# Layer 1's attention output product: seven fp32 quarter products become three fp32r products of split operands

## The chip, the cores and the metric

The kernel runs on one core of one Trainium2 chip. The metric is the device time of one execution in microseconds (us); the time before is the median of three runs. Five engines take their instructions in order, each from a queue of its own: TensorE (PE in the profile; PEld is its weight load), VectorE (DVE), ScalarE (ACT), GpSimd (POOL) and SyncE (SP), which here only issues DMAs. They wait for each other by semaphores. The order of the instructions on each engine is that in which the program issues them (`tc.manual_schedule()`).

## What is computed

Two transformer layers with AdaLN over `x` of shape 4 x 512 x 512 in fp32. Layer 0 has a small attention and a masked linear layer. Layer 1 has a causal attention with 32 query heads in 8 groups, each group with one key and value head of 128 columns, and an FFN with integer weights. The change touches layer 1's attention:

```python
q = (hidden_states @ w_q).reshape(B, S, Hkv, g, D)
k = (hidden_states @ w_k).reshape(B, S, Hkv, D)
v = (hidden_states @ w_v).reshape(B, S, Hkv, D)
scores = jnp.einsum('bqhgd,bkhd->bhgqk', q, k) * scale
probs = jax.nn.softmax(jnp.where(causal, scores, -jnp.inf), axis=-1)
attn = jnp.einsum('bhgqk,bkhd->bqhgd', probs, v).reshape(B, S, Hq * D)
return attn @ w_o
```

with B = 4, S = 512, Hkv = 8, g = 4, D = 128; `w_o` is 4096 x 512. The last line is the output product.

## The kernel before

**Blocks, pairs and windows.** Layer 1's attention runs in 32 blocks `n` (L1411): batch `n // 8`, group `n % 8`, four query heads. Two heads make a pair, and one window (L1299) handles a pair: window `2n` is a block's first half, `2n + 1` its second. Window `w` computes the scores of pair `w + 1` and the values of pair `w`, and it fills TensorE with pieces of other products from a list, `fill`, spread over slots 0 to 8 by their costs (`LONG` 1.87, `SHORT` 0.94, `SEVENTH` 1.73): a piece comes in the first slot by whose end its middle is reached.

In slot `i` a window issues, in this order: the transposition of tile `i - 2` on VectorE (`flip`); the division of tile `i - 1` (`divide`: reciprocal on VectorE, multiplication on ScalarE); the score of tile `i` (`score`: product on TensorE, mask and row maximum on VectorE, exponent on ScalarE); in slot 0 `scale_last`; in slots 8 and 9 the values of the pair's two heads (`value`: product on TensorE, eviction on ScalarE); the pieces of `fill`; what `at_slot` names; and the weight steps of `steps`. The eight tiles of a pair have 512, 384, 256, 128 columns, twice. After slot 9, `carry` (L1066) issues 16 DMAs on SyncE that move the pair's probabilities into the layout of the next window's values.

**Split operands.** q, k and v are computed as three fp32r products. A weight w becomes hi, w times a factor a little under one and rounded to fp32r, and lo = w - hi, times 4096. The activation is split in the same way into H, L and a difference D. Piece x (L921, L970) sums hi H + lo L and is evicted by ScalarE; then GpSimd subtracts lo from hi (`less`, L325), and piece p (L936, L983) multiplies what is left with D; VectorE adds it. For q and k, a piece belongs to one head or key and reads 128 columns of hi and lo; each `less` covers one head. For v, x and p belong to two tiles of rows each; both `less` come after the second x, and each covers half the weights' rows.

**Weight steps.** A step (L306) splits one staged tile of 128 x 512 weights: hi on ScalarE, lo on GpSimd, then `scale_last` (the 4096 of the step before, on ScalarE), then the load of a further tile on SyncE into one of four `raw` buffers:

```python
        nc.scalar.mul(hi, w, BELOW)
        nc.gpsimd.tensor_tensor(lo, w, hi.bitcast(F32), SUB)
        scale_last()
        scales.append(((kind, n), lo))
        stage()
```

Three tiles are staged ahead, so a step's load takes the buffer that the step before has just read. Two steps make one operand: `qa` and `qb` (two heads of q each), `k` or `v` (for two blocks). The order is that of `units` (L284): per block k or v, then qa, then qb. In a usual block the steps stand in slots 7 and 8 of the first half (k or v) and in slots 2, 4, 6, 8 of the second.

**The output product.** `o_pieces` (L992) is a 2 x 2 scheme with seven products instead of eight (`seven`, L863): each of the seven pieces multiplies quarters of the block's attention result `oT` and of its 512 rows of `w_o` (`wo`, loaded by one DMA of 1 MB, L232), or sums of quarters, in plain fp32. The sums take four operations on the left (`sums_o`, L882) and four on the right (`sums_wo`, L343), all on GpSimd. A piece is 4 products of 128 x 128 by 128 x 256, shown as 8 instructions. VectorE adds each piece to its own of seven accumulators in `osum` (L880), over the 8 groups of a batch; `leave_attention` (L1123) then combines the seven (7 operations on GpSimd), multiplies by a gate (VectorE) and adds to x (GpSimd).

In a usual block the first half's `fill` holds the four pieces of qa, the four of qb, and the p pieces of k or v begun before; the second half's holds the seven output pieces of block `n - 1` and the x pieces of k or v. After the last block a tail runs its output product, and the FFN follows.

## Time and profile before

| | us |
|---|---|
| three runs | 1956.79, 1956.91, 1956.03; median 1956.79 |
| profiled execution | 1957.64 |
| its span, first to last instruction | 1955.2 |
| windows of layer 1's attention | 168 to about 1620 |
| two windows of block 16 | 910.82 to 932.44, 932.44 to 956.84 |
| layer 0 and setup / FFN | before 168 / from 1641 on |

How to read the profile: a row of a group or of the order of time has the line of the kernel, engine, operation, `out<-in` by the program's names, shapes and a count. In the order of time the first number is the start in us from the span's start, the second the length of the merged row; the bracket at its end is idle time of the engine ahead of it, and who ended it. Product ends are modelled, so rows of TensorE overlap: differences of starts are surer. An fp32 product appears as two instructions, an fp32r one as one (its type is shown as f32 too). SPq rows are DMA issues of SyncE, with the time from issue, or from the start of a wait for its buffer, to the end of the issue. Rows on the tiles `x` and `p` of the names "x<-p" and "x<-x" at L1077 are the moves of `carry`. The table of stages gives, for each stretch, its length, then for PE, PEld, DVE, ACT and POOL the busy time with the number of instructions, the granted clock of TensorE, the DMA share and GB/s.

### The profile page before, as it was taken

To read this page: it belongs to the slowest core of one execution; us is meant where nothing else is said; L and a number is where in the kernel's file an instruction comes from. 1 tells how busy PE (TensorE), PEld (TensorE's weight loads), DVE (VectorE), ACT (ScalarE), POOL (GpSimd) and SP (SyncE) were. 2 spreads that over 40 slices of the span, in tenths; PEclk is the share of its full clock that TensorE was granted. 3 is DMA by queue.
4 is the path that set the end of the run, shared out by engine and by line. 5 is a ranking of instruction groups with operands and counts; after the bars stand their busy time and mean duration, and the time that the engine had idled before them with its cause. 6 is when DMAs were issued, how large, how long until landed. Compare 5 with 4: busy or idle time off the path is not lost.

```text
span 1955.2 us, 27500 instructions
## 1 busy us (share of the span) xinstructions
PE 1926.8 (99%) x8543; PEld 1463.0 (75%) x8543; DVE 1189.5 (61%) x3134; ACT 1101.2 (56%) x2535; POOL 969.9 (50%) x778
## 2 busy tenths in 40 slices
PE   6999999999999999999999999999999999999998
PEld 3446777777777777777777777777777777888887
DVE  7876656656656565565566656656555564755554
ACT  5426766666666666666566666666666562332322
POOL 3335555555558555555675555558555544611010
PEclk9999999999999999999999999999999999999999
DMA  9323555555555556555555555455445456401000
GB/s 326 113 71 120 157 148 165 156 153 146 142 161 162 165 145 161 147 156 151 157 162 169 152 157 136 127 151 160 130 129 156 117 140 230 154 29 36 22 23 23
DMA packets 171932, 269.07 MB, mean 138 GB/s; under 512 B 27266, under 2 KB 95938, under 8 KB 171780
## 3 DMA queue, kind: packets, MB, share of 16 engines
q1 hardware_dynamic: 171252, 266.69, 48.1%
q8 instruction: 71, 1.16, 0.2%
q14 instruction: 81, 0.66, 0.1%
q10 hardware_dynamic: 528, 0.55, 0.1%
HBM read 142.99 MB, written 11.57 MB: 79 GB/s over the span
## 4 chain that ended last, share of the span: by engine, by line
PE 93%; DVE 3%; POOL 1%; SPq 1%; ACT 1%; DMA 1%; issue 1%; POOLq 0%; DVEq 0%
PE quarter L871 20%; PE x L928 15%; PE av L1094 14%; PE sc L1034 14%; PE p L911 9%; PE p_gate L1627 5%; PE p_up L1627 5%; PE acc L1646 4%; PE x L911 3%; PE ffn L761 2%; PE lnT L606 1%; DMA wm<-in_L_wmod_dram 0%; PE narrow L379 0%; PE ffn L765 0%; DVE acc L1131 0%
## 5 line engine op out<-in xcount | busy, mean ns | idle before, releaser
L1037 DVE CUSTOM_DVE_ANT_0 sc<-sc,mask 128x512 f32<-128x512 f32 (+3 forms) x512 | 249.7, 488 | 255.9 <-PE sc L1034 255.9
L1034 PE MATMUL sc<-kT,qT 128*128 128x512 f32 (+3 forms) x1024 | 358.4, 432 | 0.0
L1094 PE MATMUL av<-x,v 128*128 128x512 f32 x1008 | 291.8, 432 | 0.0
L1094 PEld LDWEIGHTS av<-x,v 128*128 128x128 f32 x1008 | 188.3, 189 | 108.4 <-issue 60.8
L1051 ACT ACTIVATE p<-p,sums 128x512 f32<-128x512 f32 (+3 forms) x256 | 143.2, 559 | 128.1 <-DVE sums L1050 127.1
L1034 PEld LDWEIGHTS sc<-kT,qT 128*128 128x128 f32 x1024 | 186.1, 190 | 28.5 <-issue 0.7
L316 POOL TENSOR_TENSOR lo_qa<-raw,hi_qa 128x512 fp32r<-128x512 f32 x64 | 82.6, 1291 | 239.3 <-ACT hi_qa L315 210.4
L997 DVE TENSOR_TENSOR acc<-acc,quarter 128x512 f32<-128x512 f32 x196 | 134.5, 686 | 109.3 <-PE quarter L871 109.1
L1051 ACT ACTIVATE x<-x,sums 128x512 f32<-128x512 f32 (+3 forms) x256 | 142.9, 558 | 81.2 <-DVE sums L1050 81.2
L871 PEld LDWEIGHTS quarter<-wo,oT 128*128 128x128 f32 x720 | 136.5, 190 | 48.5 <-issue 24.4
L871 PE MATMUL quarter<-wo,oT 128*128 128x256 f32 x720 | 170.1, 379 | 0.0
L1054 DVE STREAM_TRANSPOSE p<-p 128x512 f32<-128x512 f32 (+3 forms) x256 | 129.2, 505 | 46.1 <-ACT p L1051 46.0
L1040 ACT ACTIVATE x<-sc,sums 128x512 f32<-128x512 f32 (+3 forms) x256 | 133.4, 521 | 42.2 <-DVE sums L1037 38.7
L1054 DVE STREAM_TRANSPOSE x<-x 128x512 f32<-128x512 f32 x248 | 125.5, 506 | 37.0 <-ACT x L1051 36.4
L1040 ACT ACTIVATE p<-sc,sums 128x512 f32<-128x512 f32 (+3 forms) x256 | 132.0, 516 | 16.2 <-DVE sums L1037 14.5
L316 POOL TENSOR_TENSOR lo_qb<-raw,hi_qb 128x512 fp32r<-128x512 f32 x64 | 82.1, 1284 | 112.3 <-ACT hi_qb L315 108.7
L940 DVE SCALAR_TENSOR_TENSOR qT<-p,qT 128x512 f32<-128x512 f32 x128 | 88.0, 690 | 78.4 <-PE p L911 78.4
L1099 ACT COPY oT<-av 128x512 f32<-128x512 f32 x128 | 74.4, 582 | 85.2 <-PE av L1094 85.2
L326 POOL TENSOR_TENSOR hi_qa<-hi_qa,lo_qa 128x512 fp32r<-128x512 f32 x64 | 82.4, 1288 | 73.0 <-PE x L928 72.7
L326 POOL TENSOR_TENSOR hi_kv<-hi_kv,lo_kv 128x512 fp32r<-128x512 f32 x64 | 81.7, 1290 | 74.2 <-PE x L911 42.6
L326 POOL TENSOR_TENSOR hi_qb<-hi_qb,lo_qb 128x512 fp32r<-128x512 f32 x64 | 82.4, 1287 | 63.2 <-PE x L928 63.2
L871 PE MATMUL quarter<-so,soT 128*128 128x256 f32 x480 | 113.5, 379 | 0.0
(271 smaller groups left out, 4239.3 us busy)
## 6 DMA issues: line engine op xcount, KB each, us to landing
x<-p SPq DMA_DIRECT2D x510, 104.0 KB, 2.2
x<-x SPq DMA_DIRECT2D x493, 104.0 KB, 2.2
raw<-in_L_attn_w_q_dram SPq DMA_DIRECT2D x128, 256.0 KB, 2.9
wo<-in_L_attn_w_o_dram SPq DMA_DIRECT2D x30, 1024.0 KB, 5.7
wm<-in_L_wmod_dram SPq DMA_DIRECT2D x12, 1024.0 KB, 9.9
raw<-in_L_attn_w_k_dram SPq DMA_DIRECT2D x32, 256.0 KB, 3.6
raw<-in_L_attn_w_v_dram SPq DMA_DIRECT2D x32, 256.0 KB, 5.0
xn<-x_d SPq DMA_DIRECT2D x28, 256.0 KB, 4.3
```

Source lines behind the costliest of these rows:

```text
L316: nc.gpsimd.tensor_tensor(lo, w, hi.bitcast(F32), SUB)
L326: nc.gpsimd.tensor_tensor(hi, hi.bitcast(F32), lo.bitcast(F32), SUB)
L871: nc.tensor.matmul(ps[:, m, :], l[:, k, m * P : (m + 1) * P], r[:, k, :], start=(k == 0), stop=(k == 1),)
L911: nc.tensor.matmul(ps[:, m * width : (m + 1) * width], still(l, k, m), moving(r, k), start=(i == 0 and k == 0), stop=(i == len(pairs) - 1 ...
L928: nc.tensor.matmul(banks[j], l[:, k, cols], r[:, k, :], start=(half == k == 0), stop=(half == 1 and k == KC - 1),)
L1034: nc.tensor.matmul(ps[:, :w], q[:, i * P : w], kT[n][:, :w], start=True, stop=True)
L1037: nc.vector.tensor_tensor_reduce(ps[:, :w], ps[:, :w], mask[:, S - w :], -1.0, -NEG, ADD, ALU.min, nmx)
L1040: nc.scalar.activation(blocks(s, i), ps[:, :w].rearrange("p (k j q) -> p k j q", j=NG, q=BK), AF.Exp, bias=nmx, scale=-1.0, accum_out=den,)
L1051: nc.scalar.mul(p, p, rden)
L1054: nc.vector.transpose(blocks(s, i), blocks(s, i))
L1094: nc.tensor.matmul(av.rearrange("p (a i q) -> p a i q", a=NG, q=BK)[:, :, k:], vs[n][:, k, :], moving(k), start=(k == 0), stop=(k == NT - 1),)
L1627: nc.tensor.matmul(ps[kind], w[kind][:, k, c * P : (c + 1) * P], h2[b % 2][i][:, k, :], start=(k == 0 and i == 0), stop=(k == KC - 1 and i ...
```

## The change

The output product takes the form that q, k and v have. The eviction of a value now writes a high part `oH` (ScalarE) and a low part `oL` (VectorE) instead of `oT`; `between_o` makes the difference `oD` on VectorE from the two, head by head, at slot 0 of the two following windows. The rows of `w_o` pass through the weight steps: four more tiles a block, split by ScalarE and GpSimd, and four `less` after the last x piece. `o_pieces` has four x pieces (8 fp32r products of 128 x 128 by 128 x 512) and four p pieces (4 each), one for each tile of 128 rows, all added to one accumulator by VectorE. The sums of quarters, the seven accumulators and their combination go.

The order of the weights becomes k or v, qb of the next block, the output's four, qa of the block after next. A usual block has steps in slots 1, 3, 5, 7, 9, 9 of its first half and 1, 3, 5, 7 of its second. The first half's pieces are qa's and the output's of block `n - 1`; the second half's are qb's and all four of k or v, so their p pieces follow in the same window. In the blocks 6, 14 and 22 the split of the next batch's activations (`swap`) takes a place in the list, and the p pieces of k follow in the next window, at its start. The last block's output product is done in two parts of two heads. One step of layer 0's order (`cs`) is issued earlier.

```diff
@@ -275,6 +240,8 @@
     def unit(kind, n, u):
 
         g = n % HKV
+        if kind == "o":
+            return a["L1_attn_w_o"][g * GW + u * P : g * GW + (u + 1) * P, :]
...
@@ -285,9 +252,16 @@
 
         yield from ((kind, 0, u) for kind in ("k", "qa", "qb", "v") for u in range(2))
         yield from ((kind, 1, u) for kind in ("qa", "qb") for u in range(2))
-        for n in range(NBLK - 2):
-            yield from (("vk"[n % 2 == 0], n // 2 + 1, u) for u in range(2))
-            yield from ((kind, n + 2, u) for kind in ("qa", "qb") for u in range(2))
+        yield from ((kind, n, u) for kind, n in (("k", 1), ("qa", 2)) for u in range(2))
+        yield from (("o", 0, u) for u in range(G))
+        for n in range(1, NBLK):
+            if n + 2 < NBLK:
+                yield from (("vk"[n % 2 == 0], n // 2 + 1, u) for u in range(2))
+            if n + 1 < NBLK:
+                yield from (("qb", n + 1, u) for u in range(2))
+            yield from (("o", n, u) for u in range(G))
+            if n + 2 < NBLK:
+                yield from (("qa", n + 2, u) for u in range(2))
...
+            dst = w if key[0] == "o" else w.rearrange("p (k n) -> p k n", n=W2)
+            nc.sync.dma_start(dst, unit(*key))
...
+        tag = kind if kind[0] in "qo" else "kv"
+        size = KC * W2
+        if kind == "o" and n + 1 == NBLK:
+            tag, n, u = ("qa", "qb")[u // 2], (n, u // 2), u % 2
+        elif kind == "o":
+            size = G * E
         if (kind, n) not in forms:
             forms[kind, n] = tuple(
-                T["wp"].tile([P, KC * W2], F32R, tag=f"{i}{tag}", name=f"{i}_{tag}")
+                T["wp"].tile([P, size], F32R, tag=f"{i}{tag}", name=f"{i}_{tag}")
...
+    def rows_o(n, h):
+
+        u = h
+        if n + 1 == NBLK:
+            n, u = (n, h // 2), h % 2
+        assert all(key != ("o", n) for key, _ in scales), n
+        return [f[:, u * E : (u + 1) * E] for f in forms["o", n]]
...
-    Lt.3 wl lm.3 le.3 F.1.2 ws ld.3 fs.2.0 fa.0.3/d F.2.1/mm hit.3 qs.3 fs.1.2 cs rs ws re fa.2.0/d
+    Lt.3 wl lm.3 le.3 F.1.2 ws ld.3 fs.2.0 fa.0.3/d F.2.1/mm hit.3 cs qs.3 fs.1.2 rs ws re fa.2.0/d
...
-    def seven(still, moving, take, order):
-
-        def piece(i):
-            l, r = still()[i], moving()[i]
-            tiles = l.shape[2] // P
-            ps = bank([P, tiles, r.shape[2]], "quarter")
-            for m in range(tiles):
-                for k in range(2):
-                    nc.tensor.matmul(
-                        ps[:, m, :], l[:, k, m * P : (m + 1) * P], r[:, k, :],
-                        start=(k == 0), stop=(k == 1),
-                    )
-            take(i, ps)
-
-        return [(SEVENTH, lambda i=i: piece(i)) for i in order]
...
+    osum = accp.tile([P, NT + NT // 2, E], F32, tag="acc", name="acc")
+    oH, oL, oD = {}, {}, {}
+
+    def between_o(n, h):
+        if n not in oD:
+            oD[n] = at.tile([P, G, S], F32R, tag="Do", name="o_df", bufs=1)
+        nc.vector.scalar_tensor_tensor(
+            oD[n][:, h], oL[n][:, h].bitcast(F32), -STEP, oH[n][:, h].bitcast(F32), ALU.mult, ADD
...
+    def o_pieces(n, all_heads=tuple(range(G))):
+
+        first_ = n % HKV == 0 and all_heads[0] == 0
+
+        def sums(t, pairs, name):
+            ps, rows_ = bank([P, 512], name), slice(t * P, (t + 1) * P)
+            for i, (l, r) in enumerate(pairs):
+                for h in all_heads:
+                    nc.tensor.matmul(
+                        ps, l[:, h, rows_], rows_o(n, h)[r],
+                        start=(i == 0 and h == all_heads[0]),
+                        stop=(i == len(pairs) - 1 and h == all_heads[-1]),
+                    )
+            return ps
+
+        def x(t):
+            ps = sums(t, ((oH[n], 0), (oL[n], 1)), "x")
+            if first_:
+                nc.scalar.mul(osum[:, t], ps, ONE)
             else:
-                nc.vector.tensor_tensor(osum[:, i - 1], osum[:, i - 1], ps, ADD)
-
-        order = (1, 2, 4, 7, 5, 6, 3) if n + 2 != NBLK else (1, 2, 3, 7, 5, 6, 4)
-        order = (1, 7, 6, 2, 4, 5, 3) if n % HKV == 0 else order
-        return seven(lambda: left["o", n], lambda: right["o", n], take, order)
+                nc.vector.scalar_tensor_tensor(osum[:, t], ps, ONE, osum[:, t], ALU.mult, ADD)
+            if t == NT - 1:
+                for h in all_heads:
+                    less(*rows_o(n, h))
+
+        def p(t):
+            ps = sums(t, ((oD[n], 0),), "p")
+            nc.vector.scalar_tensor_tensor(osum[:, t], ps, -TINY, osum[:, t], ALU.mult, ADD)
+
+        c = len(all_heads) / G
+        return [(c * LONG, lambda t=t: x(t)) for t in range(NT)] + [
+            (c * SHORT, lambda t=t: p(t)) for t in range(NT)
+        ]
...
-            oT[n] = at.tile([P, G, S], F32, tag="oT", name="oT")
+            oH[n] = at.tile([P, G, S], F32R, tag="Ho", name="o_hi", bufs=1)
+            oL[n] = at.tile([P, G, S], F32R, tag="Lo", name="o_lo", bufs=1)
...
-        nc.scalar.copy(
-            oT[n][:, h, :].rearrange("p (i a q) -> p a i q", a=NG, q=BK),
-            av.rearrange("p (a i q) -> p a i q", a=NG, q=BK),
-        )
+        H, L = (t[n][:, h, :].rearrange("p (i a q) -> p a i q", a=NG, q=BK) for t in (oH, oL))
+        av = av.rearrange("p (a i q) -> p a i q", a=NG, q=BK)
+        nc.scalar.mul(H, av, BELOW)
+        nc.vector.tensor_tensor(L, av, H.bitcast(F32), SUB)
...
+        dfs = [[lambda h=h: between_o(n - 1, h) for h in (2, 3)] if behind else []]
+        dfs.append([lambda h=h: between_o(n, h) for h in (0, 1)])
...
-            sums, ends = leave_attention(b - 1, nc.gpsimd, gap, "ga", xb)
-            in_b = {8: sums[:3]}
+            ends = leave_attention(b - 1, nc.gpsimd, gap, "ga", xb)
+            in_b = {0: ends[:1], 2: ends[1:3], 4: ends[3:5], 6: ends[5:7], 7: ends[7:]}
...
-            window(2 * n, o[:2] + t[:2] + [r[0]] + o[2:3] + t[2:3] + [r[1]] + t[3:] + [r[2]] + o[3:4] + [r[3]] + o[4:])
+            fill = o[:2] + t[:1] + o[2:4] + t[1:2] + r[:1] + t[2:3] + r[1:2] + o[4:5] + t[3:] + r[2:3]
+            fill += o[5:6] + r[3:] + o[6:]
+            window(2 * n, fill, (), (1, 3, 5, 7, 8), {0: dfs[0]})
             warm = small.tile([P, 1], F32, tag="warm", name="warm", bufs=1)
             nc.scalar.activation(warm, ones[:, 0:1], AF.Sigmoid)
 
-            last = [f for _, f in o_pieces(n)]
-            s = at.tile([P, 3, 2, HALF], F32, tag="soT", name="soT", bufs=1)
-            A11, A21, A12, A22 = quarters(oT[n])
-            left["o", n] = {1: A11, 2: A12, 3: s[:, 2], 4: A22, 5: A21, 6: s[:, 1], 7: s[:, 0]}
-            nc.vector.tensor_tensor(s[:, 0], A11, A21, SUB)
-            run(last[0], last[3])
+            run(*dfs[1])
+            head, tail = (o_pieces(n, hs) for hs in ((0, 1), (2, 3)))
+            run(*(f for _, f in head[:4]))
             value(NBLK * G - 2)
             value(NBLK * G - 1)
-            nc.vector.tensor_tensor(A21, A21, A22, ADD)
-            nc.vector.tensor_tensor(s[:, 1], A21, A11, SUB)
-            nc.vector.tensor_tensor(s[:, 2], A12, s[:, 1], SUB)
-            run(*last[1:3], *last[4:])
+            run(*(lambda h=h: between_o(n, h) for h in (2, 3)))
+            run(*(f for _, f in head[4:] + tail))
...
-        so = sums_o(n - 1) if n > 0 else 4 * [(0.0, lambda: None)]
-        wo = [(0.0, lambda: sums_wo(n - 1))] if n > 0 else []
         if n == 0:
             window(0, begun[:1] + qa[:1] + begun[1:] + qa[1:] + qb[:1], side[0], (1, 7, 8), {3: [scale_last]}, (9, 9))
         else:
-            fill = begun[:1] + qa[:1] + so[:1] + qa[1:2] + begun[1:] + so[1:2] + qb[:1] + qa[2:3] + so[2:3]
-            fill += qb[1:2] + so[3:] + qa[3:] + wo + qb[2:]
-            window(2 * n, fill, side[0], (7, 8) if more and n % HKV != 1 else (), in_a)
+            fill = begun + qa[:1] + o[:4] + qa[1:3] + o[4:] + qa[3:]
+            early_ = (0, 1, 2, 3, 5, 7) if n == 1 else (1, 3, 5, 7) if more else (1, 3)
+            if n == 1:
+                fill = begun + qa + o
+            in_a.setdefault(0, []).extend(dfs[0])
+            window(2 * n, fill, side[0], early_ + (9, 9), in_a)
...
+        swap = []
         if g == HKV - 2 and after:
             h3[after] = H, L, D
-            for c in range(KC):
-                in_b.setdefault(c, []).append(lambda c=c: (upper(h3[after], spare, c), lower(h3[after], spare, c)))
-                in_b.setdefault(c + 1, []).append(lambda c=c: between(h3[after], c))
+            swap = [(0.0, lambda c=c: (upper(h3[after], spare, c), lower(h3[after], spare, c))) for c in range(KC)]
...
-        fresh = (2, 3, 7, 8) if n == 0 else (0, 1) * (n % HKV == 1) + (2, 4, 6, 8)
-        window(2 * n + 1, (qb[1:] if n == 0 else o) + kv[:2], turns_ + side[1], fresh if more else (), in_b)
-        begun = kv[2:]
+        in_b.setdefault(7 if n == 0 else 0, []).extend(dfs[1])
+        fresh = (2, 3, 6, 7) if n == 0 else (1, 3, 5, 7)
+        late = 2 if n == 0 or swap else len(kv)
+        window(2 * n + 1, (qb[1:] if n == 0 else qb + swap) + kv[:late], turns_ + side[1], fresh, in_b)
+        begun = kv[late:]
...
```

Not shown: the removal of `load`, `quarters`, `left_sums`, `right_sums`, `load_parts`, `rooms`, `sums_wo`, `sums_o`, of the old `o_pieces` and of the seven sums in `leave_attention`; where the last pair's transposed probabilities lie (`straight_of`); names of buffers.

## The prediction, on record before the result was known

> **What bounds the kernel now.** I read the page's top first, then two stages of the attention in the table of stages, then TensorE's order of time, then the queues of ScalarE, GpSimd and SyncE around one border of two windows.
>
> ```profile
> span 1955.2 us, 27500 instructions
> PE 1926.8 (99%) x8543; PEld 1463.0 (75%) x8543; DVE 1189.5 (61%) x3134; ACT 1101.2 (56%) x2535; POOL 969.9 (50%) x778
> PE 93%; DVE 3%; POOL 1%; SPq 1%; ACT 1%; DMA 1%; issue 1%; POOLq 0%; DVEq 0%
> ```
>
> TensorE is the bound. The profiled execution took 1957.64 us: its span and 2.4 us around it; it is 0.85 us over the median of the three timed runs, 1956.79. The table of stages shows windows 32 and 33 (block 16) with no idle TensorE at all (length, then each engine's busy time):
>
> ```profile
> 910.82:932.44 21.62, 21.62 (x99) 16.35 (x97) 12.44 (x38) 13.36 (x33) 16.47 (x14) 1.00 0.59 165
> 932.44:956.84 24.40, 24.40 (x107) 19.09 (x106) 13.55 (x41) 15.38 (x37) 10.23 (x9) 1.00 0.59 167
> ```
>
> The clock is 1.00. A saving on TensorE therefore counts in full, and so does any wait that the change brings it. TensorE's order of time gives the prices; I take them from start to start, since the modelled ends overlap:
>
> ```profile
> 915.12 0.59 PE L1034 MATMUL sc<-kT,qT 128*128 128x256 f32 x2
> 915.37 1.28 PE L928 MATMUL x<-h_hi,hi_qa 128*128 128x512 f32 x4
> 916.48 1.09 PE L928 MATMUL x<-h_lo,lo_qa 128*128 128x512 f32 x4
> 917.41 0.38 PE L1034 MATMUL sc<-kT,qT 128*128 128x128 f32 x2
> ...
> 933.30 1.89 PE L871 MATMUL quarter<-wo,oT 128*128 128x256 f32 x8
> 935.02 0.81 PE L1034 MATMUL sc<-kT,qT 128*128 128x384 f32 x2
> ```
>
> A quarter product is 935.02 - 933.30 = 1.72. Scores take 0.86, 0.65, 0.43 and 0.22 for 512 to 128 columns (932.44 to 933.30 is the first). So an x piece, two of the three products, is 917.41 - 915.12 - 0.43 = 1.86 (others 1.83), and a p piece, the third, 0.94 (925.12 to 926.28 less 0.22).
>
> **The saving.** Per block, 7 quarters at 1.725 = 12.08 go; 4 x at 1.84 and 4 p at 0.935 = 11.1 come. That is 0.98 less, for 31 blocks (the first has no output product behind it; the last one's runs in the tail): **-30 us**. Without new waits a first-half window would be 25.4 us and a second-half one 19.9.
>
> **Work that lies beside TensorE.** GpSimd loses 8 sums per block (soT, oT, so, wo rows) and gains 4 splits and 4 subtractions for the output weights, all at 1.28 to 1.30: 10.3 for 10.3. ScalarE gains 8 passes at 0.62, one every 0.52: 28.7 busy of 46 becomes 33 of 45. VectorE loses 7 sums at 0.69 and gains 4 low parts, 4 differences, 8 accumulations: 26 becomes 32. SyncE issues four loads of 256 KB (0.4 to 0.5 each) where it issued one of 1 MB (0.58). No engine's sum becomes the bound; leave_attention's 7 sums on GpSimd and the cselb move (rsel waits 1.1 us for it now) are worth 1 us at most. What counts is where the new steps stand in the queues.
>
> **The queues as the trace shows them.** ScalarE, GpSimd and SyncE over the border at 932.44, after a window whose last two weight steps stood at its end:
>
> ```profile
> 929.12 0.64 ACT L315 ACTIVATE hi_kv<-raw 128x512 fp32r<-128x512 f32 x1
> 933.58 0.63 ACT L304 ACTIVATE lo_kv<-lo_kv 128x512 fp32r<-128x512 f32 x1 [3.82 <-POOL lo_kv L316]
> 934.11 0.57 ACT L1099 COPY oT<-av 128x512 f32<-128x512 f32 x1
> 934.58 0.69 ACT L1040 ACTIVATE p<-sc,sums 128x512 f32<-128x512 f32 x1
> 935.16 0.20 ACT L1040 ACTIVATION_READ_ACCUMULATOR p<-sc,sums 128x1 f32 x1
> 935.25 0.63 ACT L304 ACTIVATE lo_kv<-lo_kv 128x512 fp32r<-128x512 f32 x1
> ```
> ```profile
> 932.27 2.51 POOL L316 TENSOR_TENSOR lo_kv<-raw,hi_kv 128x512 fp32r<-128x512 f32 x2
> ```
> ```profile
> 922.89 11.05 SPq L298 DMA_DIRECT2D raw<-in_L_attn_w_q_dram  x2
> 934.05 1.15 SPq L1077 DMA_DIRECT2D x<-x  x2
> ```
>
> The second step's scale_last blocks ScalarE until GpSimd's first low part is done (933.54); the exponent of the new window goes ahead of the last scale; the raw load waits 10 us for that same low part, and the 16 moves of the probabilities stand behind it, 1.6 us late. Today it costs nothing: quarters follow. The change moves two steps behind the last value (slot 9, twice) and puts the q, k and v pieces right behind.
>
> **Wait 1, start of the first half, from F.** The block's last step (slot 7 of the window before) splits the second half of the weights of qa, and its scale comes only at the window's start, behind the exponent. qa's first x piece stands in slot 0 and reads that low part with its seventh matmul: F + 0.86 + 6 x 0.23 = 2.25. ScalarE: eviction of the second value from F + 0.20 (911.02 after 910.82), 0.59; VectorE's new low part, 0.61 to the next start; maximum 0.70 + 0.14; exponent 0.68; scale 0.62, ends at F + 3.6. Wait 1.3. Ends: 0.9 (if the maximum could start at 1.06 as at 911.88), 1.5 (a weight load of 0.19 behind it). Blocks 2 to 30 but the 3 after a swap, where k's p pieces lie first: 26 x 1.3 = **+34**.
>
> **Wait 2, second half, from E.** ScalarE: eviction E + 0.2, hi, scale, hi up to 2.24; wait for GpSimd's low part (1.37 to 2.64); scale to 3.2; exponent to 3.88; second scale (low part done 3.91) to 4.5; x eviction, division, exponent to 6.13; hi of slot 1's step to 6.75. GpSimd: that low part to 8.1, and only then the subtraction for qb's second head, to 9.4. Its p piece is due at 0.86 + 1.86 + 0.65 + 0.43 + 1.86 + 0.22 + 0.94 + 0.86 = 7.7. Wait 1.7. Even if GpSimd were in time, the moves would not be: the raw load waits for 2.64, the moves start at 3.2, 16 at 0.635 end at 13.4 and land 2.2 later, 15.6, and the first value is due at 14.6: 1.0. Above, the two new differences of low and high part on VectorE, both read from SBUF, meet GpSimd there. The view of line 1131, the gate, also two such inputs:
>
> ```profile
> L1131 DVE TENSOR_TENSOR acc<-acc,ga x16: 678/1602/1783, 608.6 to 1675.3; 128x512 f32<-128x512 f32 x16
> ```
>
> Alone it takes 0.68, beside GpSimd's work mostly 1.6. Two such collisions delay the low part and then the division by some 0.55: 2.3. I take 2.0; ends 1.0 and 2.5. Windows of blocks 1 to 29: 29 x 2.0 = **+58**.
>
> The Trainium skill, "SBUF — State Buffer", section "Who interferes with whom", says that a VectorE instruction with two SBUF inputs shuts out a GpSimd instruction that reads SBUF, and the reverse, for a whole instruction. The row agrees (0.68 against 1.60); it speaks against this change, whose 128 new differences are all of that kind. With the rule in full wait 2 is 2.3 (29 x 2.3 = 67 us), without it 1.7 (49 us).
>
> **Wait 3, second half, blocks with v (odd).** v's two subtractions follow its second x piece; now they run at 908.25 to 910.75, 4.0 us after that piece began (906.7), and a value of 2.16 and a score of 0.86 cover them. Afterwards only a score of 0.22 lies between. p may start at 2.13, gets its first weights at 2.8 and the rest at 4.05, and ends at 4.77 instead of 3.09: 1.7. If slot 5's low part is ahead on GpSimd, 2.3. I take 1.9: 15 x 1.9 = **+28**.
>
> **Once each.** Window 2 has four steps and qa's products close together, and the output's four subtractions behind one score (+3); in the tail the last p pieces wait for two subtractions of 1.28 (+2): **+5**, ends 0 and 10. In other blocks the four subtractions need 5.0 us from the last x piece's start and 6.4 lie before the last one's use: nothing.
>
> **Sum.** No wait can fall below nothing, since TensorE never stands still now. -30 + 34 + 58 + 28 + 5 = +95 on 1957.6: 2052.6; less 0.85, about **2050 us**. All low ends: -30 + 23 + 29 + 24 + 0 = +46, 2003. All high ends: -30 + 39 + 73 + 35 + 10 = +127, 2084.
>
> **Rivals.**
> A, the other side: the waits are hidden and TensorE's sum decides, -30 + 2: 1929. For it: TensorE stands still nowhere today, and all other engines have 27% or more to spare. Against it: each wait is a chain of measured durations from a window's own border, so spare time elsewhere cannot shorten it. It decides if the three waits together come to less than 0.98 us a block, which is what a block saves.
> B: GpSimd's queue is met in a kinder order, and waits 2 (its part beyond the moves, 29) and 3 (28) go; wait 1 and the moves' 1.0 stay: -30 + 34 + 29 + 5 = +38, 1995. For it: GpSimd is busy only 58% of a block. Against it: the low part of slot 1 is issued ahead of the subtraction.
> C: the time is kept within 0.2% (what a measurement can tell from no change) because only wait 1 comes: -30 + 34, 1960.
>
> **Chances.** Forecast (2003 to 2084) 0.66, B 0.16, C 0.04 (a third of it over 0.2%), A 0.14. Faster 0.14, same 0.03, slower 0.83. With B, the range is 1975 to 2085.
>
> **What would show it.** Right: in the second product's x piece TensorE idles for the scale of lo_qa in each first-half window (about 26.7 us long); in the second half it idles at p for hi_qb and, in odd blocks, hi_kv (windows near 22 and 24 us); moves start 3 us into second halves. Wrong: windows of 25.4 and 19.9 us, TensorE without idle time.

## The result, and the profile after

The changed kernel takes **2199.89 us** (median of 4 runs, 2192.84 to 2200.85), the kernel before 1956.85 in the same comparison (4 runs, 1956.03 to 1957.54): ratio **1.1234**, 95% interval 1.121 to 1.1259. The forecast was 2050, with a range up to 2085. The profiled execution took 2198.98 us, 2.2 more than its span, and 241.3 more than the one of before.

The top of the page, and the first line of the chain that ended last:

```profile
span 2196.8 us, 27560 instructions
PE 1986.6 (90%) x8287; PEld 1436.3 (65%) x8287; DVE 1382.3 (63%) x3411; ACT 1237.7 (56%) x2808; POOL 966.6 (44%) x754
PE 14%; DVE 0%; ACT 0%; issue 0%
```

TensorE was busy for 99% of the span and is now for 90%. It has 256 instructions fewer, and still its busy time is 60 us longer. Matmuls that ran at half clock count double (107 us of the busy time lie in such stretches, 7 before), and the last product ahead of each wait counts with its whole modelled length. The granted clock over the span fell from 0.998 to 0.971.

The table of stages, with the length first, then the busy time of TensorE, its weight loads, VectorE, ScalarE and GpSimd, and the granted clock as the third number from the right. The first two rows are windows 20 and 21 (block 10), the last two windows 47 and 55:

```profile
710.48:737.20 26.72, 25.57 (x106) 18.80 (x105) 16.80 (x46) 15.20 (x36) 12.63 (x10) 1.00 0.50 133
737.20:759.43 22.23, 20.43 (x82) 14.37 (x81) 14.07 (x39) 16.41 (x40) 12.57 (x10) 1.00 0.60 157
1429.85:1454.62 24.77, 20.97 (x106) 15.79 (x105) 14.64 (x40) 17.59 (x42) 13.46 (x10) 1.00 0.47 123
1639.94:1666.36 26.42, 22.61 (x106) 16.71 (x105) 14.63 (x40) 17.59 (x42) 13.47 (x10) 0.94 0.43 115
```

The regular windows are near what the prediction wanted to see (26.7, 22 and 24). Windows 47 and 55 do the same work with the same waits, but 55 takes 1.65 longer: its clock is 0.94.

**Wait 1** in TensorE's and ScalarE's order of time, at the border 710.48. In brackets stands the idle time before an instruction and what ended it:

```profile
712.27 0.62 PE L882 MATMUL x<-h_lo,lo_qa 128*128 128x512 f32 x2
714.04 0.73 PE L882 MATMUL x<-h_lo,lo_qa 128*128 128x512 f32 x2 [1.15 <-ACT lo_qa L279]
```
```profile
712.70 0.69 ACT L1017 ACTIVATE x<-sc,sums 128x512 f32<-128x512 f32 x1 [1.42 <-DVE sums L1014]
713.28 0.19 ACT L1017 ACTIVATION_READ_ACCUMULATOR x<-sc,sums 128x1 f32 x1
713.37 0.62 ACT L279 ACTIVATE lo_qa<-lo_qa 128x512 fp32r<-128x512 f32 x1
```

The third matmul on the low part waits for the scale, which stands behind the exponent.

**Wait 2** in window 21, TensorE, then GpSimd, then VectorE:

```profile
744.43 1.02 PE L1011 MATMUL sc<-kT,qT 128*128 128x512 f32 x2
747.10 1.19 PE L865 MATMUL p<-h_df,hi_qb 128*128 128x512 f32 x4 [1.65 <-POOL hi_qb L306]
```
```profile
738.65 2.98 POOL L296 TENSOR_TENSOR lo_o<-raw,hi_o 128x512 fp32r<-128x512 f32 x2 [5.49 <-issue]
741.59 1.74 POOL L306 TENSOR_TENSOR hi_qb<-hi_qb,lo_qb 128x512 fp32r<-128x512 f32 x1
744.54 1.27 POOL L296 TENSOR_TENSOR lo_o<-raw,hi_o 128x512 fp32r<-128x512 f32 x1 [1.22 <-ACT hi_o L295]
745.77 1.27 POOL L306 TENSOR_TENSOR hi_qb<-hi_qb,lo_qb 128x512 fp32r<-128x512 f32 x1
```
```profile
739.24 2.93 DVE L837 SCALAR_TENSOR_TENSOR o_df<-o_lo,o_hi 128x512 fp32r<-128x512 f32 x2
```

The second subtraction for qb stands behind the low part of slot 1's step (744.54). While VectorE makes its two differences (2.93), the first subtraction takes 1.74; the later one, alone, 1.27.

**Wait 3** in window 55, TensorE, then GpSimd:

```profile
1655.77 0.39 PE L1011 MATMUL sc<-kT,qT 128*128 128x128 f32 x2
1657.40 0.50 PE L865 MATMUL p<-hi_kv,h_df 128*128 128x256 f32 x2 [1.25 <-POOL hi_kv L306]
1658.64 1.47 PE L865 MATMUL p<-hi_kv,h_df 128*128 128x256 f32 x6 [0.74 <-POOL hi_kv L306]
```
```profile
1654.83 1.30 POOL L296 TENSOR_TENSOR lo_qa<-raw,hi_qa 128x512 fp32r<-128x512 f32 x1 [3.56 <-ACT hi_qa L295]
1656.09 2.50 POOL L306 TENSOR_TENSOR hi_kv<-hi_kv,lo_kv 128x512 fp32r<-128x512 f32 x2
```

v's two subtractions stand behind the low part of slot 5's step (1654.83), and v's first p piece waits for each of them in turn.

**Where the time went.** I went through TensorE's order of time from start to start, gave each instruction its usual price, called what is left over a wait for the operand that the view names, and kept the half-clock stretches apart. The prices are medians, so a term is good to 1 or 2 us. Over the spans (+241.6):

| term | predicted | measured |
|---|---|---|
| work saved | -30 | -29 |
| wait 1 | 34 | 39 |
| wait 2 | 58 | 74 |
| wait 3 | 28 | 39 |
| window 2, waits | 3 | 11 |
| window 62 and tail | 2 | 18 |
| other waits | 0 | 50 |
| half clock, up to window 61 | 0 | 44 |
| before window 2, FFN | 0 | -4 |

The other waits have places of their own. At three batch ends (windows 17, 33, 49) VectorE stood 10 us for a load, and TensorE 5.1 to 5.5 of these behind VectorE. TensorE, VectorE and SyncE in window 17:

```profile
647.06 2.07 PE L882 MATMUL x<-h_hi,hi_kv 128*128 128x512 f32 x4 [5.47 <-DVE qT L894]
```
```profile
644.97 0.69 DVE L1114 TENSOR_TENSOR acc<-acc,ga 128x512 f32<-128x512 f32 x1 [10.00 <-DMA ga<-rows]
```
```profile
630.82 10.08 SPq L1057 DMA_DIRECT2D x<-x  x16
640.94 0.59 SPq L154 DMA_DIRECT2D ga<-rows  x1
```

The gate's row is asked for at the second half's start, but SyncE issues the 16 moves first. In window 62 ScalarE stood 10.5 us for a low part that GpSimd could not make, since its casts of the FFN's first weights, ahead in its queue, waited 17.2 for their load:

```profile
1836.34 1.29 POOL L1267 CAST first<-raw 128x512 fp32r<-128x512 int32 x2 [17.20 <-DMA raw<-in_L_ffn_gate_wqT_dram]
1842.18 2.48 POOL L296 TENSOR_TENSOR lo_qb<-raw,hi_qb 128x512 fp32r<-128x512 f32 x2
```

Further: in blocks 3, 11, 19 and 30 o's first p piece waits 3.0 us. A layer norm stands in VectorE's and ScalarE's queues there (L1142, L1154), so ScalarE is late with the hi of slot 3's step; its low part is ahead of o's four subtractions on GpSimd, which begin 16.3 us into window 6 and 13.1 into the regular window 20. Behind the three swaps of the batch the first x piece of k waits 1.5 to 2.4. In window 61 the value product waits 4.9 for the moves.

### The profile page after: what moved, and what is told of

The parts are those of the page before. It is cut to its first block, busy times and chain, and to the rows that moved or that the text cites. A ratio compares the mean times of both kernels' runs of the same rounds, so it can differ in the third digit from the quotient of the medians.

```text
span 2196.8 us, 27560 instructions
## 1 busy us (share of the span) xinstructions
PE 1986.6 (90%) x8287; PEld 1436.3 (65%) x8287; DVE 1382.3 (63%) x3411; ACT 1237.7 (56%) x2808; POOL 966.6 (44%) x754
## 5 line engine op out<-in xcount | busy, mean ns | idle before, releaser
L1075 PE MATMUL av<-x,v 128*128 128x512 f32 x1008 | 312.1, 455 | 4.9 <-DMA x<-x 4.9
L296 POOL TENSOR_TENSOR lo_o<-raw,hi_o 128x512 fp32r<-128x512 f32 x124 | 172.0, 1398 | 238.0 <-issue 144.6
L1083 DVE TENSOR_TENSOR o_lo<-av,o_hi 128x512 fp32r<-128x512 f32 x128 | 88.3, 690 | 226.8 <-ACT o_hi L1082 226.5
L1082 ACT ACTIVATE o_hi<-av 128x512 fp32r<-128x512 f32 x128 | 76.0, 597 | 218.7 <-PE av L1075 218.7
L954 PE MATMUL x<-hi_o,o_hi 128*128 128x512 f32 x496 | 165.1, 455 | 1.2 <-ACT acc L964 1.2
L954 PE MATMUL p<-hi_o,o_df 128*128 128x512 f32 x496 | 145.5, 422 | 14.7 <-POOL hi_o L306 14.0
L296 POOL TENSOR_TENSOR lo_kv<-raw,hi_kv 128x512 fp32r<-128x512 f32 x64 | 83.3, 1302 | 169.4 <-ACT hi_kv L295 161.6
L306 POOL TENSOR_TENSOR hi_o<-hi_o,lo_o 128x512 fp32r<-128x512 f32 x124 | 155.7, 1287 | 3.2 <-PE x L954 3.2
L954 PE MATMUL x<-lo_o,o_lo 128*128 128x512 f32 x496 | 133.7, 391 | 0.0
L865 PE MATMUL p<-h_df,hi_qb 128*128 128x512 f32 x256 | 78.7, 429 | 58.8 <-POOL hi_qb L306 57.7
```

The costliest lines, as they stand in the source:

```text
L306: nc.gpsimd.tensor_tensor(hi, hi.bitcast(F32), lo.bitcast(F32), SUB)
L954: nc.tensor.matmul(ps, l[:, h, rows_], rows_o(n, h)[r], start=(i == 0 and h == all_heads[0]), stop=(i == len(pairs) - 1 and h == all_heads ...
L1075: nc.tensor.matmul(av.rearrange("p (a i q) -> p a i q", a=NG, q=BK)[:, :, k:], vs[n][:, k, :], moving(k), start=(k == 0), stop=(k == NT - 1),)
L1083: nc.vector.tensor_tensor(L, av, H.bitcast(F32), SUB)
```

## The experiments

Two theories stood at first. **A**: each wait is a matter of order, goes when the late work is put earlier or the asking later, and the clock's halves follow from the waits. **B**: the forms can't be made faster by the engines behind TensorE, so a wait taken away comes back at the next place. The expectations use their own letters: the W of e1 and e2 is A; rival A of e1 and E of e5 say that the new products, or their load, lower the clock; C and D belong to e4 and e5 alone.

**e1, wait 1 alone.** The scale of lo_qa at the end of the window before:

```diff
+        if n > 0:
+            in_b.setdefault(9, []).append(scale_last)
```

> Changed kernel, with the scale of the last weight step issued in slot 9 of the second half, ahead of the next window's exponent. Theory W (the loss is waits in the order of the queues): the wait of qa's first x piece, 1.43 us in 27 first halves, goes and nothing takes its place: 39 us less, about 2160; first halves 25.3 instead of 26.7. Rival A (fp32r products of this shape, or the load they put on TensorE, are slow in themselves and lower its clock): no wait moves the time, within 8 us of 2200.

2159.67 us, 40 less, as W said. The same kind of first half, TensorE, without the wait; such a window takes 25.30:

```profile
1582.27 1.49 PE L882 MATMUL x<-h_hi,hi_qa 128*128 128x512 f32 x4
1583.60 1.08 PE L882 MATMUL x<-h_lo,lo_qa 128*128 128x512 f32 x4
```

Wait 1 is order alone: nothing came back.

**e2, wait 2 alone.** The second half's steps one slot later:

```diff
-        fresh = (2, 3, 6, 7) if n == 0 else (1, 3, 5, 7)
+        fresh = (2, 3, 6, 7) if n == 0 else (2, 4, 6, 8)
```

> Changed kernel, with the second half's steps in slots 2, 4, 6, 8 instead of 1, 3, 5, 7, so that the subtraction of qb's second head is ahead of a split on GpSimd. Theory W: wait 2 falls from 2.4 to 1.0 or less (the moves of the probabilities are then what is late), 29 x 1.4 = 40 less; wait 3 falls from 2.5 to 1.7 in 15 windows, 12 less; with the clock's share 10 to 20 more: 2130 to 2150. Rival B (the second half is short of GpSimd's or ScalarE's time as a whole): the wait moves to another piece of the same window, within 10 us of 2200.

2145.91 us, 54 less. The two subtractions now run back to back on GpSimd (1646.60 to 1649.6), and qb's second p piece has no wait in view:

```profile
1646.60 3.01 POOL L306 TENSOR_TENSOR hi_qb<-hi_qb,lo_qb 128x512 fp32r<-128x512 f32 x2
1651.38 1.28 POOL L296 TENSOR_TENSOR lo_o<-raw,hi_o 128x512 fp32r<-128x512 f32 x1 [1.78 <-DMA x<-x]
```

Added up, wait 2 fell from 74 to 12 us and wait 3 from 39 to 31; x pieces of k and v at batch ends and swaps rose by 15, k's p pieces by 7. So the step's low part ahead of the subtraction was the cause; some 30% of the gain came back, as B says.

**e3, the p pieces of k and v a window later.**

```diff
-        late = 2 if n == 0 or swap else len(kv)
+        late = 2
```

> The two p pieces of k or v always stand at the start of the next block's first half, as they already do at n = 0 and at the batch ends. Theory A (wait 1 is there because qa's first x piece opens the first half; wait 3 is there because v's p piece comes right behind its x pieces): both go, 39 + 39 us by the trace of the changed kernel, and the p pieces of k and v at the new place wait some 0.8 us each for hi_kv, 30 places, +24 at most; with less idle time the clock's share of 44 shrinks by some 10. Together about 2199 - 60 = 2140 us, between 2120 and 2160. Rival theory (the work that is late is late wherever it is asked for): 2190 to 2210.

2141.99 us, as A said: waits 1 and 3 both go (78 us), and new ones come: k's p pieces +8, scores at the batch ends 15, and value products that wait for the moves 13, since the second half is now only 21 to 22 us long.

**e4, the collision of VectorE and GpSimd.** The second half's two differences at slot 4:

```diff
-        in_b.setdefault(7 if n == 0 else 0, []).extend(dfs[1])
+        in_b.setdefault(7 if n == 0 else 4, []).extend(dfs[1])
```

> Changed kernel, with the second half's two differences on VectorE in slot 4 instead of slot 0. Theory C (SBUF inputs of VectorE and GpSimd shut each other out at the border): wait 2 falls from 2.4 to about 1.8, 29 x 0.6 = 17 less, 2180. Rival: the chain of ScalarE sets it alone, wait 2 stays 2.4, within 5 us of 2200.

2216.08 us, 16 *more*: both numbers missed. The collision itself did go. GpSimd at the start of one second half, with the first subtraction at 1.31 and not 1.74, and VectorE's two differences in another, 1.28 and not 2.93:

```profile
1710.70 2.52 POOL L296 TENSOR_TENSOR lo_o<-raw,hi_o 128x512 fp32r<-128x512 f32 x2 [5.50 <-issue]
1713.18 1.31 POOL L306 TENSOR_TENSOR hi_qb<-hi_qb,lo_qb 128x512 fp32r<-128x512 f32 x1
```
```profile
1668.75 1.28 DVE L837 SCALAR_TENSOR_TENSOR o_df<-o_lo,o_hi 128x512 fp32r<-128x512 f32 x2
```

Wait 2 fell by some 15 us, 0.5 per window: that is the collision's share of it. (In window 21 ScalarE waits 0.39 for the second low part, which holds up the hi of slot 1's step; here that wait is gone.) But everything behind slot 4 became later: wait 3 rose by 9, the x pieces of k and v at batch ends and swaps by 8, k's p pieces by 8, the half clock by 7. B holds in this run.

**e5, the clock.** Eight products that nobody reads, ahead of qb's second p piece and of v's first one, where TensorE would wait:

```diff
+        def spin(piece):
+            ps, hs = ps_av.tile([P, 512], F32, tag="av", name="spin"), h3[b][0]
+            for k in range(2 * KC):
+                nc.tensor.matmul(ps, hs[:, k % KC, :P], hs[:, k % KC, :], start=True, stop=True)
+            piece()
```

> Changed kernel, with 8 products more (1.87 us of TensorE, into a bank that nobody reads) ahead of qb's last p piece in the second halves, and 8 more ahead of v's first p piece: inside waits 2 and 3 (2.4 and 2.5). The output stays the reference's. Theory D (TensorE's clock is halved for 3.4 or 6.8 us where it stood still too long): the added work costs nothing and keeps the clock at 1: 44 us are lost to the clock now, some 25 to 35 of them after these two waits, so 2165 to 2180. Rival E (the clock falls because of load): the time does not fall, 2200 or more.

2188.57 us: with more work the kernel is 11 us faster, though D's 2165 to 2180 is missed. A regular second half with v, which took 24.8 to 25.0 or 26.4 to 26.7, now takes 24.8 to 25.1; only windows 11, 27 and 43 take longer (27.0, against 29.5 to 29.8):

```profile
1628.54:1653.38 24.84, 24.26 (x122) 18.73 (x121) 14.65 (x40) 17.60 (x42) 13.53 (x10) 1.00 0.46 123
```

The half clock's cost fell from 44 to 22 us; half of that was lost again in places where the eight products are longer than the wait or meet none (window 61 grew from 22.0 to 26.1). Idle TensorE, not the new products, lowers the clock: e11, with all the new products and few waits, has no half-clock stretch at all from window 2 to window 61.

**e6, the two late loads.**

```diff
-            in_b = {0: ends[:1], 2: ends[1:3], 4: ends[3:5], 6: ends[5:7], 7: ends[7:]}
+            in_a.setdefault(4, []).extend(ends[:1])
+            in_b = {2: ends[1:3], 4: ends[3:5], 6: ends[5:7], 7: ends[7:]}
...
-            first_weights()
...
-            window(2 * n, fill, (), (1, 3, 5, 7, 8), {0: dfs[0]})
+            window(2 * n, fill, (), (1, 3, 5, 7, 8), {0: dfs[0], 9: [first_weights]})
```

> Two DMAs asked for earlier or later, nothing else: the gate's row of a finished batch is loaded in the block's first half and not behind the 16 moves of the second half's start, and the first weights of the next stage are loaded and cast at the end of the last window but one. Theory A (at three batch ends VectorE waits 10 us for that row, and TensorE 5.4 of these through k's x piece; and in window 62 TensorE waits 10 us for casts that GpSimd holds back): 3 x 5.4 + 10 and the clock's halves around them, some 8: 2199 - 34 = 2165, between 2155 and 2180. Rival theory (these stalls only show time that another wait would take anyway): within 8 us of 2199.

2166.97 us, 33 less, as theory A said.

**e7, all at once.** e1, e2 and e6, `late = 2`, and these orders of pieces:

```diff
+            fill = qa[:1] + begun + o[:4] + qa[1:2] + o[4:] + qa[2:]
...
+            fill = begun + qa[:2] + o[:4] + qa[2:] + o[4:]
...
+            fill = qb[:2] + kv[:1] + qb[2:] + kv[1:2]
```

> All places at once: the scale of lo_qa at the end of the second half, the second half's steps one slot later, k's first x piece between qb's x and p pieces, the p pieces of k and v in the next first half behind qa's first x piece, the gate's row earlier, the casts later, window 2 with o's x pieces ahead of qa's p pieces. Theory A (the change is worth 30 us of TensorE work and everything else is waits that are a matter of order): the windows without a wait give 1927, and what is left is window 2 (some 8), block 30's moves (5), the swaps (5) and a dozen waits under 0.5 us, with a little clock: 1945 to 1985. Rival theory (the engines behind TensorE, GpSimd with the shared port above all, can't deliver the forms at this pace): over 2040.

2123.74 us: in the rival's range (over 2040) and far from A's 1945 to 1985, but not for the rival's reason. Waits 1, 2 and 3 were gone and GpSimd held up little (18 us, most of it at o's p pieces), but a new one stood in every second half, 106 us in all. TensorE and SyncE of window 21:

```profile
721.04 0.38 PE L1011 MATMUL sc<-kT,qT 128*128 128x128 f32 x2
724.90 2.40 PE L1075 MATMUL av<-x,v 128*128 128x512 f32 x8 [3.48 <-DMA x<-x]
```
```profile
712.31 0.38 SPq L273 DMA_DIRECT2D raw<-in_L_attn_w_q_dram  x1
712.82 10.25 SPq L1057 DMA_DIRECT2D x<-x  x16
```

The half is now 18 us of work, and TensorE reaches the value product 12 us into it. The moves start 3.3 us into it, because a raw load ahead of them waits for GpSimd, and take 10.2.

**e8 and e9, two ways round the moves.** Both put the two value products behind all pieces; e8 issues 4 of the 16 moves on ScalarE's queue, e9 takes the p pieces of k and v back into the second half:

```diff
+        aside = {0: 2, 1: 3, 2: 0, 61: 6}.get(pair, 4 * (pair % 2))
```

> The kernel with all waits out, whose second halves then waited 3.5 us each for the last of the 16 moves of the exponentials (one queue issues them, 0.63 us each). Here ScalarE's queue issues 4 of the 16 in second halves, both value products come behind all of the half's pieces, the steps of the first half stand at slots 1, 2, 5, 7, and the first half behind a swap begins with k's p pieces. Theory A (the moves are the next bound: they can't start before the last value product of the half before has read its tile, and take 10.1 us + 2): 4 moves fewer take 2.5 us off, k's second x piece ahead of the value products another 1.9, so the wait goes: 2124 - 106 and of the clock's 49 most: 1965 to 2010. Rival theory (what ends late is the transfers themselves, not their issue on one queue): the moves still land at the same time and only the 1.9 us of the moved piece are won, 30 x 1.9 + some clock: 2040 to 2070.

> As the run beside it, but the 16 moves stay on one queue, and the p pieces of k and v go back to the second half, behind qb's: work instead of the wait for the moves. Theory A: the second half has 16.3 us of pieces and scores ahead of the value products, 15.3 are needed; what comes back is v's p piece waiting for GpSimd, 1 to 1.7 us in 15 blocks, and k's by some 0.5: 1960 to 2010 with the clock. Rival theory (as beside): the same, since here the transfers' end is hidden by work: it can't tell them apart by itself, only the pair can.

2111.30 and 2045.76 us, both over what was expected, e8 even over its rival's 2040 to 2070. In e8 the wait for the moves went, but issuing is not free on ScalarE: 3.85 us for four, and the first exponent stands behind it:

```profile
712.72 3.85 ACTq L1057 DMA_DIRECT2D x<-x  x4
716.68 0.69 ACT L1017 ACTIVATE p<-sc,sums 128x512 f32<-128x512 f32 x1 [3.39 <-DMA x<-x]
```

In e9 no regular half waits for the moves, and wait 3 is back (2.1 in blocks with v); in those with k the p piece waits 0.8, now for ScalarE's kT.

**e10, the moves first at the border.** e7, with the first half's last two steps at slot 8 in place of 9 and its second one a slot earlier, the value products behind all pieces, and two of o's x pieces first behind a swap:

> The kernel with all waits out, with three changes of order and the moves on one queue again: the first half's last two steps stand at slot 8 and not 9, so that no load of raw weights waits on SyncE's queue ahead of the 16 moves at the border; both value products of second halves come behind all pieces; the first half behind a swap begins with two of o's x pieces. Theory A (the wait for the moves is a matter of 1.3 us by which the load ahead of them is late and of 1.9 us by which k's second x piece stood behind the wait): no wait for the moves is left in the regular blocks; with window 2 (6), the swaps (3 x 3), block 30 (6) and some clock 1950 to 1990. Rival theory (a half of 18 us is too short for the moves' 10.1 us, the flips before them and the landing behind them, whatever the order): 1 to 2 us a block stay, with the clock's halves 2010 to 2060.

2007.37 us. A regular second half has no wait left: SyncE starts the moves 0.2 us into it, and it takes 18 us.

```profile
678.21 10.54 SPq L1057 DMA_DIRECT2D x<-x  x16
```
```profile
1487.15:1505.16 18.01, 18.01 (x90) 13.77 (x89) 12.06 (x37) 14.62 (x37) 8.44 (x7) 1.00 0.61 159
```

The total missed A's range by 17: 24 us for lo_qa's scale were not in the estimate, and the swaps, put at 9, cost 15 at o's x pieces alone. B's "1 to 2 us a block stay" at the moves is wrong.

**e11 to e14, what was left.** e11: the second half's steps at slots 1, 3, 5, 7 again, and a swap's four differences in the next first half. e12: `fill = qa[:1] + begun + o[:4] + qa[1:3] + o[4:] + qa[3:]` and other orders at the swaps, in block 30, in window 2 and in the tail. e13 and e14: window 2 alone, e13 with steps at (0, 0, 1, 2, 5, 7), e14 at (0, 0, 1, 4, 7, 8).

> The kernel with the moves first at the border, with two changes of order: the second half's steps at slots 1, 3, 5, 7 again (so qa's lower form is done a slot sooner), and behind a swap of the batch the four differences of the new x are made in the next first half, where the first p piece asks for them, and not in the second half. Theory A (what was left at 2007 are waits of order: 24 us for lo_qa's scale in first halves, 15 us behind the three swaps, 9 us of clock behind these): 24 and 12 of these go, with the clock some 6: 1960 to 1975; the work alone would give some 1935. Rival theory (the forms can't be made faster: what is won at lo_qa comes back at qb's p pieces as wait 2): 1990 to 2010.

> The kernel with the forms earlier (1968), with what its trace still shows as waits put in another order: qa's first p piece ahead of o's p pieces in first halves (some 25 waits of 0.2 us for GpSimd, 5); in window 2 qa's first x piece first and one step two slots later (6 of waits, some 4 of them); behind a swap one x piece of o between the differences and k's p pieces, and the swap's and block 30's second halves with later steps (1.9 x 3 + 1.5 x 3 + 2); at the very end the second two heads' x pieces between the first two heads' p pieces (2). Theory A (order is all that is left, and the new products' own work is 0.75 us a block shorter than the seven): 1968 - 17 = 1951, between 1946 and 1957, so level with the kernel before or up to 0.5% faster. Rival theory (each of these waits hides another one behind it): 1963 to 1970.

> The kernel ordered all over, with window 2 the other way round again (k's p pieces first, o's x pieces ahead of qa's p pieces) and its first steps earlier (slots 0, 0, 1, 2, 5, 7 and the last scale at slot 3), so that o's lower forms are there when its first x piece is. Theory A (window 2's 39 us, 11.6 more than its work, were the order's fault, 6 of them o's p pieces behind GpSimd's four subtractions; with the regular blocks at 45.1 against 46.1 the whole is level with the kernel before): window 2 falls to 29 to 32, 1965 - 8 = 1957, between 1953 and 1960. Rival theory (window 2 can't be faster, since the weights of o and v come late from memory): window 2 stays above 33, 1960 to 1966.

> As the run before, with the last three single steps of window 2 at slots 4, 7, 8 in place of 2, 5, 7, and the scale before them at slot 2. The trace of the run before shows why window 2 stayed at 35.4: ScalarE stood 6.0 us in its second step on v for a load of raw weights that SyncE issues behind the 16 moves, and o's x pieces stood 4.1 behind ScalarE. Theory A (order again): the 4.4 us for o's x piece go, the clock's 1.4 in that window too, and 1 of the 1.5 for lo_o: 1960 - 6 = 1954, between 1951 and 1957, level with the kernel before or 0.2% faster. Rival theory (the late load only moves the wait to qb's forms in window 3, whose steps now come last): 1957 to 1962.

1968.50, 1965.20, 1959.82 and 1960.91 us, with ratios 1.0061 (1.0047 to 1.0074), 1.0048 (1.0034 to 1.0061), 1.0018 (1.0009 to 1.0027) and 1.0022 (1.0012 to 1.0031). e11 hit. e12 missed A and lies in its rival's range, but for the most part because its own order of window 2 made that window 39.0 us long (33.6 in e11). e13 is just inside A's range, while its window 2 took 35.4 and not 29 to 32, over the 33 that the rival named; e14 lies in its rival's range, with a window 2 of 36.3. In e13 ScalarE stands in window 2 for a load that SyncE issues behind the moves:

```profile
237.94 0.63 ACT L295 ACTIVATE hi_kv<-raw 128x512 fp32r<-128x512 f32 x1 [5.96 <-DMA raw<-in_L_attn_w_v_dram]
```

e14 cut that to 2.3, and o's p pieces waited some 4 us there instead. The regular block of e12 and e13 is without any wait; the row pair of e12 (block 28) and the one of the kernel before:

```profile
1468.84:1495.96 27.12, 27.12 (x122) 20.88 (x121) 19.23 (x49) 17.43 (x40) 16.88 (x14) 1.00 0.42 112
1495.96:1513.84 17.88, 17.88 (x74) 12.95 (x73) 12.22 (x37) 15.24 (x38) 10.21 (x9) 1.00 0.78 208
```
```profile
1463.82:1485.44 21.62, 21.62 (x99) 16.35 (x98) 12.44 (x38) 13.36 (x33) 16.47 (x14) 1.00 0.52 140
1485.44:1509.84 24.40, 24.40 (x107) 19.09 (x106) 12.51 (x39) 15.45 (x37) 9.47 (x8) 1.00 0.60 167
```

45.00 against 46.02 us. No version beat the kernel before: e13 comes within 0.2% of it. The irregular blocks (window 2, swaps, batch ends, tail) cost what the regular ones save: in e13 blocks 2 to 30 together are 8 us shorter than in the kernel before, and block 1 alone is 8.7 longer. Whether they could be ordered better was not tried further.

## Why the prediction was wrong, step by step

- **The saving** (0.98 us a block) was right: 1.02 in e12. So were the windows without a wait: 25.4 against 25.30 (e1).
- **Wait 1**: mechanism right, 1.3 against 1.42 (26.72 less 25.30). e1 settles it.
- **Wait 2**: mechanism right, 2.0 against 2.4. The step chose a middle value; e4 shows the collision's share (0.5 a window), so the 2.3 with "the rule in full" was the better one. The Trainium skill's "SBUF — State Buffer", "Who interferes with whom", has such a pair of instructions contend; the rows agree in that both engines lose time (1.74 against 1.27 and 2.93 against 1.28). But of the 128 new differences only 50 took over 1.1 us, the other 78 some 0.65: the kind alone does not decide, the moment does. And the 0.68 that the step read as "alone" is one row, beside which a GpSimd row began 0.16 later and took 1.68.
- **The moves** behind wait 2 ("Even if GpSimd were in time, the moves would not be", 1.0): hardly seen in e2, where the regular halves keep 21 to 22 us and the value products wait 2 us more in all; real in e7, where the half holds 18 us of work.
- **Wait 3**: mechanism right, 1.9 against 2.5. The prediction's own 2.3, for slot 5's low part ahead on GpSimd, was nearer, and the rows show that part ahead (1654.83).
- **"Once each", +5**: failed, 29. Window 2 and the tail were priced by their pieces, not by following each queue; the casts ahead of a low part were in the code.
- **"In other blocks the four subtractions ... nothing"**: failed in blocks 3, 11, 19, 30, where the layer norm's work holds up the low part ahead of them (3.0 us each). The 50 us of other waits are nearly all in blocks that differ from the regular one, and the prediction followed the queues only through a regular one.
- **"The clock is 1.00. A saving on TensorE therefore counts in full, and so does any wait"**: failed. A wait cost more than itself: 44 us, which no step priced. This and the irregular blocks are most of the 147 us by which the sum fell short; the three waits' sizes are 32.
- **Rival A** ("spare time elsewhere cannot shorten" a wait, said against it) was wrong for this order of work, but an order exists in which most of the waits go (e13, 1959.8, still not A's 1929). B (1995) and C (1960) lay further off than the forecast.

## What to carry to other kernels

A kernel whose TensorE never waits hides how late everything else is: before new readers of a buffer are put close behind its writers, follow each in-order queue, the DMA queue too, through one block of *every* kind (first, batch end, swap, last) and not only the regular one. Price a wait on TensorE with its clock: 2 us of idle time that fall together cost window 55 1.65 more. And when waits are taken out one by one, expect the next bound (here the 16 moves) before the sum is reached.

## What the runs showed of the hardware

In the changed kernel's trace all stretches of half clock begin on one grid of 3.413 us and last one or two of its steps (but for one of four in window 62 and the last, which the program's end cuts off). Four neighbouring steps of that grid in window 55:

```profile
1652.04:1655.46 3.42, 3.42 (x29) 3.37 (x29) 1.76 (x6) 3.11 (x7) 0.64 (x1) 1.00 0.57 134
1655.46:1658.87 3.41, 1.43 (x10) 1.03 (x10) 0.93 (x4) 3.04 (x9) 3.41 (x4) 1.00 0.90 289
1658.87:1662.28 3.41, 3.41 (x10) 2.07 (x10) 1.09 (x3) 0.40 (x1) 0.95 (x1) 0.50 0.02 6
1662.28:1665.70 3.42, 3.42 (x18) 2.50 (x17) 1.51 (x3) 0.60 (x1) 0.00 (x0) 1.00 0.00 0
```

TensorE idles 1.98 us of one step and gets half the clock in the next. From 120 us on in that trace, every drop but the last, at the program's end, follows a step with at least 1.9 us idle (TensorE's order of time cut at the grid's lines, each instruction at its usual price), and no step at full clock with more than 2.2 idle goes without one. What makes some stretches two steps long stays open. The grid does not follow the program's windows: in window 47 the same wait (1445.9 to 1448.5) falls on both sides of a grid line, 1447.2, and no drop comes. The Trainium skill, "TensorE: Matmul & The Clock Gate", Part 1, has a free-running activity window of 3413 ns and half rate after an idle one; the length agrees, but here 2 us of idle time in a window were enough.

Issuing a move took 0.63 us on SyncE's queue (10.08 for 16) and 0.96 on ScalarE's (3.85 for 4).
